# Half-slot order in a three-layer graph kernel: counts one half at a time, table remainders behind a maximum, VectorE's pieces half a slot behind their products

## The chip, the cores and the metric

The kernel runs on one core of one Trainium2 chip. The time is the device time of one execution in microseconds (us); the median of three runs counts. A core has a matrix engine (TensorE, PE in the profile), a vector engine (VectorE, DVE), a scalar engine (ScalarE, ACT), a general-purpose engine (GpSimd, POOL) and a queue engine for transfers (SyncE, SP). Each engine carries out its own instructions in order, and semaphores hold an instruction until what it reads or overwrites is ready. PSUM, where the matrix engine writes its products, has 8 banks of 512 float32 values per partition.

## The reference

Four layers work on 16 graphs of 1024 nodes with 128 features. Each is `x = layernorm(x + layer(x, adj))`.

- Layer 0 is attention over neighbours: relu of three linear maps, scores `q k^T` with non-neighbours pushed down by a penalty, a softmax, and a sum of `v`.
- Layer 1 is an edge convolution with a maximum over neighbours:

```python
p = jnp.einsum('bnd,do->bno', x, W1 - W2)
q = jnp.einsum('bnd,do->bno', x, W2)
pre = p[:, :, None, :] + q[:, None, :, :] + b
h = jax.nn.relu(pre) * adj[..., None]
return jnp.max(h, axis=2)
```

- Layer 2 adds up neighbours and applies a two-layer network with a relu.
- Layer 3 first thins out the adjacency row by row: a row with many neighbours loses every few of them, with the symmetric entries, so that later rows see what earlier ones removed (the dilation). Then come three mean aggregations with a normalisation of rows and batch statistics over all graphs, and a last linear map.

## The kernel before

The maximum over neighbours is the bulk of the work. It is the maximum of `q` over the neighbours, plus `p`. The kernel takes the source nodes of a graph in groups of 12 (`PS`), two sets of 6. For each set it makes a **table** of the maxima of `q` over all 64 subsets of the six nodes (`tables_of`, on VectorE, tile `sub`). Which subset a node sees is found by a product of the adjacency with signs (`count`, L701 to L709): TensorE counts matches into `pm` (L708), ScalarE turns that into a one-hot `hot` (L709). A second product of `hot` with the table picks the maximum out (`look_up`, L737, tile `pg`), and VectorE takes the running maximum over groups (`best`, L789 and L791). A table is cut into a rounded part `high` and a remainder `low`, and both are multiplied. So each table first goes through a transpose on TensorE (`pt`, L720), a cast on ScalarE (`high`, L722) and a subtraction on VectorE (`low`, L728), for two groups at once.

One graph has 86 groups (`NP`), and 16 graphs make 1376 **slots**, one group each. The order of the instructions on each engine is written out by this program itself (`slot`, from L749), not by a scheduler. A slot has two halves, of 512 nodes each. In each half it writes, in this order: four matmuls of the look-up, then what other **streams** have for TensorE, then what they have for the other engines (`advance`), and last the maximum. The counts and the table for the slot after next are written in the second half, behind the streams, both halves of the counts together. The subtraction `low` stands at the start of every odd slot.

The streams are generators: `scores` and `attend` (layer 0 and the products of layer 1 for the next graph), `rest` (end of layer 1 and layer 2 for the graph before), `tables_of`, and beside them `dilation`, which is paced by due times counted in slots. A stream yields what it wants next with `ask(engine, cost, ...)`. `advance` lets it go on if its engine has room, if the delay since its last step has passed, and, for a product (`take=True`), if one of two shared PSUM banks is free. The delay is half a slot, or none with `same=True`. A piece with `give=True` reads a product out of its bank, and the bank may be taken again half a slot later. The pieces of VectorE that the change touches read products in this way: `e` (scores, L330), `y` (L379, L396, L441) and `hT` (L420).

There are two PSUM pools of note. `wide` has two tiles of two banks for `pg`, so the look-up of one half waits until the maximum of two halves before has read its tile. `subset` has two banks, which `pm` and `pt` use in turn in the order in which they are asked for: three in an even slot and two in an odd one. The remainder `low` reads `pt` too, so `pt`'s bank comes free when `low` is done.

When the slots are over, the last pieces of the dilation and the aggregations of layer 3 follow, without slots.

Of the kernel before, what the change touches and what calls it, by code (L numbers as in the profile page):

```python
# [71 lines left out]
def tile_graph_layers(ctx: ExitStack, tc, a, out):  # L72
# [161 lines left out]
    def layers_012():  # L234
# [56 lines left out]
        def scores(b):  # L291

            if b > 1:
                yield ask("Pool", 0, after=("p", b - 1))
            if b > 2:
                yield ask("Pool", 0, after=("rest", b - 3))
            load_rows(b)
            xT = w4.tile([P, N], F32, name="xT")
            yield from columns_of(xT, X[b])
            qT = w4.tile([P, N], F32, name="qT")  # L300
            yield from product_of(WqT, xT, qT, AF.Relu, bq)
            kT = w4.tile([P, N], F32, name="kT")
            yield from product_of(WkT, xT, kT, AF.Relu, bk)
            v = values[b] = w4.tile([P, T, D], F32, name="v")
            for h in range(2):
                yield ask("PE", 1.1, take=True)
                pv = shared("pv").rearrange("p (t d) -> p t d", d=D)
                nc.tensor.matmul(pv, ones_b[:3, :], four(bv3), start=True, stop=False)
                for t in range(4):
                    nc.tensor.matmul(pv[:, t, :], xT[:, (4 * h + t) * P:(4 * h + t + 1) * P], WvT,  # L310
                                     start=False, stop=(t == 3))
                yield ask("A", 0.6, give=True, same=True)
                nc.scalar.activation(v[:, 4 * h:4 * h + 4, :], pv, AF.Relu)
            for t in range(T):

                yield ask("A", 1.05)
                off = w4.tile([P, N], BF, name="off", tag="pen")
                nc.scalar.activation(off, An[b][:, t, :], AF.Identity, bias=ones[:, 0:1], scale=-1.0)
                if t > 1:
                    yield ask("PE", 0, same=True, after=("back", b, t - 2))  # L320
                e = w4.tile([P, N], F32, name="e", bufs=2)

                tops = small.tile([P, 2], F32, name="tops")
                for h, s in enumerate(halves):
                    yield ask("PE", 1.07, take=True)
                    psc = shared("psc")
                    nc.tensor.matmul(psc, qT[:, t * P:(t + 1) * P], kT[:, s], start=True, stop=False)  # L327
                    nc.tensor.matmul(psc, penalty, off[:, s], start=False, stop=True)
                    yield ask("V", 0.66, give=True, same=True)
                    nc.vector.tensor_scalar(e[:, s], psc, CLAMP_HI, None, op0=ALU.min, op1=ALU.max,  # L330
                                            accum_out=tops[:, h:h + 1])
                yield ask("V", 0.1, same=True)
                top = small.tile([P, 1], F32, name="top")
                nc.vector.tensor_scalar(top, tops[:, 0:1], tops[:, 1:2], -1.0, op0=ALU.max, op1=ALU.mult)
                yield ask("A", 1.1)
                total = small.tile([P, 1], F32, name="total")
                nc.scalar.activation(e, e, AF.Exp, bias=top, accum_out=total)
                exps[b, t] = e, total
                happened["e", b, t] = now
            yield ask("A", 0.01, after=("X1", b), delay=0.5)  # L340
            xT = w4.tile([P, N], F32, name="xT1", tag="xT")
            yield from columns_of(xT, X[b])
            q = w4.tile([P, NP * PS], F32, name="q", bufs=2)
            nc.gpsimd.memset(q[:, N:], LOWEST)
            yield from product_of(W01[:, 1, :], xT, q[:, :N], None, None)
            qs[b] = q
            happened["q", b] = now
            if b > 1:
                yield ask("A", 0, same=True, after=("y1", b - 2))
            p = ps[b] = w4.tile([P, N], F32, name="p", bufs=2)  # L350
            yield from product_of(Wd, xT, p, AF.Identity, b01)
            happened["p", b] = now

        def attend(b):
            for t in range(T):
                yield ask("PE", 0.01, after=("e", b, t))
                if t == 0:
                    y = w4.tile([P, T, D], F32, name="y0", tag="xT")
                e, total = exps.pop((b, t))
                eT = w4.tile([P, T, P], F32, name="eT")  # L360
                for h in range(2):
                    yield ask("PE", 0.44, take=True, same=(h == 0))
                    p = shared("pe")
                    for c in range(4):
                        nc.tensor.transpose(p[:, c * P:(c + 1) * P],  # L365
                                            e[:, (4 * h + c) * P:(4 * h + c + 1) * P], ident)
                    yield ask("A", 0.59, give=True, same=True)
                    nc.scalar.copy(eT[:, 4 * h:4 * h + 4, :].rearrange("p c i -> p (c i)"), p)  # L368
                happened["back", b, t] = now
                for h in range(2):  # L370
                    yield ask("PE", 0.9, take=(h == 0))
                    if h == 0:
                        pav = shared("pav")[:, :D]
                    for c in range(4 * h, 4 * h + 4):
                        nc.tensor.matmul(pav, eT[:, c, :], values[b][:, c, :], start=(c == 0), stop=(c == T - 1))  # L375
                yield ask("V", 0.4, give=True, same=True)
                share = small.tile([P, 1], F32, name="share")
                nc.vector.reciprocal(share, total)
                nc.vector.scalar_tensor_tensor(y[:, t, :], pav, share, X[b][:, t, :], op0=ALU.mult, op1=ALU.add)  # L379
            yield from norm(X[b], y)  # L380
            happened["X1", b] = now


        def rest(b):
# [4 lines left out]
            for h in range(2):  # L389
                yield ask("PE", 0.44, take=True)  # L390
                pt = shared("ph")
                for t in range(4):
                    nc.tensor.transpose(pt[:, t * P:(t + 1) * P],
                                        best[:, (4 * h + t) * P:(4 * h + t + 1) * P], ident)
                yield ask("V", 0.66, give=True, same=True)
                nc.vector.tensor_add(y[:, 4 * h:4 * h + 4, :], X[b][:, 4 * h:4 * h + 4, :],  # L396
                                     pt.rearrange("p (t d) -> p t d", d=D))
            happened["y1", b] = now
# [12 lines left out]
            for h, s in enumerate(halves):  # L411
                for c in range(T):
                    yield ask("PE", 0.65, take=(c == 0), same=(c > 0))
                    if c == 0:
                        pa = shared("pa")
                    for k in range(3):
                        nc.tensor.matmul(pa, parts[:, k, c, :], An[b][:, c, s], start=(c == 0 and k == 0),  # L417
                                         stop=(c == T - 1 and k == 2))
                yield ask("V", 0.66, give=True, same=True)
                nc.vector.scalar_tensor_tensor(hT[:, s], xT[:, s], eps1, pa, op0=ALU.mult, op1=ALU.add)  # L420
            del An[b]
            zT = []
# [5 lines left out]
            for h in range(2):  # L428
                q = slice(4 * h, 4 * h + 4)
                for half in range(2):  # L430
# [4 lines left out]
                    for t in range(2 * half, 2 * half + 2):  # L435
                        own = slice((4 * h + t) * P, (4 * h + t + 1) * P)
                        for k in range(2):
                            nc.tensor.matmul(py[:, t, :], zT[k][:, own], W2[:, k, :],  # L438
                                             start=False, stop=(t == 3 and k == 1))
                yield ask("V", 0.65, give=True, same=True)  # L440
                nc.vector.tensor_mul(y[:, q, :], py, nm[:, q, b].unsqueeze(2).to_broadcast([P, 4, D]))  # L441
                yield ask("V", 0.65)
                nc.vector.tensor_add(y[:, q, :], y[:, q, :], X[b][:, q, :])
# [305 lines left out]
        def slot(s, last):  # L749
# [14 lines left out]
                    start(rest(b - 1))  # L764
            if s >= 0 and g % PC == 0:
                load_columns(b * (T + 1) + g // PC + 2)
            if s % 2 and s + 1 < last:
                low_part(s + 1)
            for h in range(2):
                now = s + 0.5 * h  # L770
                if s >= 0:
# [4 lines left out]
                if h == 0:  # L776
                    while s >= 0 and due <= s and not (wants_bank and taken >= 2 and given.get(taken - 2, 1e9) > now):
                        after, cost, wants_bank = next(dilate, (B * NP, 0, False))
                        due += after
                        room["V"] -= cost  # L780
                elif s + 2 < last:
                    for half in range(2):
                        count(s + 2, half)
                    if s % 2 == 0:
                        table(s + 2)
                if s >= 0:
                    own = bests[b][:, :, halves[h]]
                    if g == 0:
                        nc.vector.tensor_copy(own, pg)  # L789
                    else:  # L790
                        nc.vector.tensor_max(own, own, pg)  # L791
            if s >= 0:
                hots.pop(s)

# [24 lines left out]
        last = rest(B - 1)  # L819
# [310 lines left out]
```

## Time and profile before

Three runs took 7400.84, 7415.03 and 7416.94 us; the median is 7415.03 us. The profiled execution has a span of 7420.3 us at a mean granted TensorE clock of 0.856.

| engine | busy us | share of the span | instructions |
|---|---|---|---|
| TensorE matmuls | 5789.6 | 78% | 26554 |
| TensorE weight loads (beside matmuls) | 2790.6 | 38% | 26554 |
| VectorE | 5516.8 | 74% | 8427 |
| ScalarE | 3510.6 | 47% | 5849 |
| GpSimd | 3475.9 | 47% | 11285 |

| group | count | mean ns | busy us |
|---|---|---|---|
| VectorE `best`, L791 | 2720 | 1212 | 3226.8 |
| ScalarE `hot`, L709 | 2752 | 684 | 1740.9 |
| TensorE `pg` with `high` / with `low`, L737 | 5504 each | 549 / 445 | 1528.6 / 1247.6 |
| TensorE `pm`, L708 | 2752 | 432 | 953.7 |
| TensorE `pt`, L720 | 1376 | 331 | 337.3 |
| VectorE `low`, L728 | 688 | 421 | 289.9 |

To read it: the busy time of matmuls overlaps and their ends are modelled, so a share of 78% doesn't say how much is left. A group's idle time is what its engine stood still for just before it, and the engine named beside it is the one whose result came last. The slots run from about 130 us to 6090 us, the rest is the tail of layer 3. The chain of work that ended last is by engine TensorE 48%, VectorE 31%, ScalarE 10%.

### The profile page before, as it was taken

To read this page: it belongs to the slowest core of one execution; us is meant where nothing else is said; L and a number is where in the kernel's file an instruction comes from. 1 tells how busy PE (TensorE), PEld (TensorE's weight loads), DVE (VectorE), ACT (ScalarE), POOL (GpSimd) and SP (SyncE) were. 2 spreads that over 40 slices of the span, in tenths; PEclk is the share of its full clock that TensorE was granted. 3 is DMA by queue.
4 is the path that set the end of the run, shared out by engine and by line. 5 is a ranking of instruction groups with operands and counts; after the bars stand their busy time and mean duration, and the time that the engine had idled before them with its cause. 6 is when DMAs were issued, how large, how long until landed. Compare 5 with 4: busy or idle time off the path is not lost.

```text
span 7420.3 us, 84498 instructions
## 1 busy us (share of the span) xinstructions
PE 5789.6 (78%) x26554; PEld 2790.6 (38%) x26554; DVE 5516.8 (74%) x8427; ACT 3510.6 (47%) x5849; POOL 3475.9 (47%) x11285
## 2 busy tenths in 40 slices
PE   6768787777777777787778787878787767888996
PEld 3323333333333333333333333333333324555653
DVE  3888888888888888888888888888888774444443
ACT  3545455555454545454545454545454443333751
POOL 3454554545555555555555555555555551110116
PEclk8878888888888888888988888889888778888998
DMA  5121212121212121212121112121111025565544
GB/s 34 18 24 18 29 19 29 19 29 18 30 18 30 18 30 18 29 18 28 18 29 18 28 18 28 17 30 20 30 18 22 14 30 104 114 114 110 191 157 153
DMA packets 494372, 318.88 MB, mean 43 GB/s; under 512 B 316651, under 2 KB 445669, under 8 KB 489829
## 3 DMA queue, kind: packets, MB, share of 16 engines
q0 software_dynamic: 105648, 84.20, 13.1%
q1 hardware_dynamic: 383600, 228.10, 10.9%
q8 instruction: 211, 3.46, 0.2%
q10 hardware_dynamic: 4676, 1.19, 0.1%
q14 instruction: 237, 1.93, 0.1%
HBM read 413.70 MB, written 118.16 MB: 72 GB/s over the span
## 4 chain that ended last, share of the span: by engine, by line
PE 48%; DVE 31%; ACT 10%; issue 5%; POOL 4%; DMA 2%; ACTq 0%; DVEq 0%; SPq 0%; POOLq 0%
PE pg L737 15%; DVE best L791 13%; ACT hot L709 6%; PE pagg L910 5%; PE pm L708 4%; DVE rank L626 4%; PE pav L375 3%; PE psc L327 3%; PE pp L284 2%; PE pa L417 2%; PE pt L720 2%; DVE sub L465 2%; DVE gone L632 2%; PE pe L365 2%; PE py L438 1%
## 5 line engine op out<-in xcount | busy, mean ns | idle before, releaser
L791 DVE TENSOR_TENSOR best<-best,pg 128x1024 f32<-128x1024 f32 x2720 | 3226.8, 1212 | 266.3 <-PE pg L737 255.5
L709 ACT ACTIVATE hot<-pm,one_less 128x512 fp32r<-128x512 f32 x2752 | 1740.9, 684 | 1967.4 <-PE pm L708 1963.9
L737 PE MATMUL pg<-hot,high 64*128 64x512 f32 x5504 | 1528.6, 549 | 689.2 <-DVE best L791 609.5
L737 PE MATMUL pg<-hot,low 64*128 64x512 f32 x5504 | 1247.6, 445 | 0.0
L737 PEld LDWEIGHTS pg<-hot,high 64*128 64x128 f32 x5504 | 592.6, 207 | 1707.5 <-issue 589.3
L708 PE MATMUL pm<-AT,lit 120*128 120x512 fp8e4 x2752 | 953.7, 432 | 8.0 <-ACT hot L709 7.3
L720 PE MATMUL pt<-ident,sub 128*128 128x128 f32 x1376 | 337.3, 331 | 482.5 <-ACT hot L709 463.7
L737 PEld LDWEIGHTS pg<-hot,low 64*128 64x128 f32 x5504 | 624.4, 219 | 12.9
L728 DVE TENSOR_TENSOR low<-pt,high 128x256 fp32r<-128x256 f32 x688 | 289.9, 421 | 368.6 <-ACT high L722 364.6
L489 POOL DMA_DIRECT2D E<-in_adj_dram x128 | 70.8, 563 | 953.2 <-DVE gone L632 856.9
L577 POOL TENSOR_SCALAR sc<-low_counts,half_mask,rest 16x1 f32<-16x1 f32 x992 | 340.2, 343 | 301.7 <-DVE rest L563 207.5
L720 PEld LDWEIGHTS pt<-ident,sub 128*128 128x128 f32 x1376 | 151.2, 154 | 877.2 <-ACT hot L709 875.6
L582 POOL TENSOR_SCALAR sc<-sc 16x1 f32<-16x1 f32 x992 | 391.9, 395 | 104.7
L708 PEld LDWEIGHTS <-lit 120*128 120x128 fp8e4 x2752 | 200.6, 101 | 518.4 <-issue 500.0
L579 POOL TENSOR_SCALAR sc<-sc 16x1 f32<-16x1 f32 x992 | 318.8, 321 | 107.5
L584 POOL TENSOR_SCALAR hit<-V,sc 16x31 bf16<-16x31 bf16 (+30 forms) x992 | 361.3, 364 | 0.0
L409 POOL TENSOR_TENSOR left<-X,parts 128x1024 f32<-128x1024 f32 x16 | 34.1, 2133 | 674.3 <-ACT parts L406 674.3
L940 POOL TENSOR_TENSOR length<-length,mhalf 128x8 f32<-128x8 f32 x48 | 79.0, 1645 | 572.1 <-DVE length L939 572.1
L629 ACT ACTIVATE rank<-rank,centre,scale 128x1024 f32<-128x1024 f32 x128 | 158.7, 1240 | 392.5 <-DVE rank L626 392.5
L585 POOL TENSOR_SCALAR last_rank<-V,sc 16x31 f32<-16x31 bf16 (+30 forms) x992 | 337.5, 340 | 0.0
L465 DVE TENSOR_TENSOR sub<-sub,q 128x24 f32<-128x24 f32 (+11 forms) x768 | 316.4, 413 | 23.8 <-ACT q L287 10.5
L375 PE MATMUL pav<-v,eT 128*128 128x128 f32 x2048 | 317.3, 303 | 2.0 <-ACT eT L368 2.0
(242 smaller groups left out, 9498.9 us busy)
## 6 DMA issues: line engine op xcount, KB each, us to landing
removed<-gone SPq DMA_DIRECT2D x128, 256.0 KB
An<-in_adj_dram POOLq DMA_DIRECT2D x16, 1024.0 KB, 14.8
E<-in_adj_dram POOLq DMA_DIRECT2D x128, 128.0 KB, 6.4
gone_all<-removed POOLq DMA_DIRECT2D x64, 256.0 KB, 12.3
near<-in_adjT_dram POOLq DMA_DIRECT2D x16, 1024.0 KB, 17.4
h<-x SPq DMA_DIRECT2D x32, 512.0 KB
kept<-near SPq DMA_DIRECT2D x16, 1024.0 KB
share<-share SPq DMA_DIRECT2D x32, 512.0 KB
```

The source lines that it names most:

```text
L375: nc.tensor.matmul(pav, eT[:, c, :], values[b][:, c, :], start=(c == 0), stop=(c == T - 1))
L465: nc.vector.tensor_max(sub[:, :n_g, n:2 * n], sub[:, :n_g, 0:n], qg[:, 2 * g0:2 * g0 + n_g, k:k + 1].to_broadcast([P, n_g, n]))
L577: gp.tensor_scalar(half, mine, half_mask[:, m], rest[:, n:n + 1], op0=ALU.mult, op1=ALU.add)
L582: gp.tensor_scalar(to, at, sf, none, op0=ALU.subtract, op1=ALU.subtract)
L584: gp.tensor_scalar(hit[:, n, n + 1:], V[:, n, n + 1:], at, None, op0=ALU.is_equal)
L585: gp.tensor_scalar(last[:, n + 1:], V[:, n, n + 1:], to, None, op0=ALU.is_le)
L708: nc.tensor.matmul(pm, lit[:, r, :], AT[b * (T + 1) + c][:, halves[h]], start=True, stop=True)
L709: nc.scalar.activation(hots[s][:, halves[h]], pm, AF.Relu, bias=one_less)
L720: nc.tensor.transpose(pt[:, k * P:(k + 1) * P], subs[b, g0][:, g - g0 + k, :], ident)
L737: nc.tensor.matmul(pg[:, a], part[rows, at * P:(at + 1) * P], hots[s][rows, halves[h]], start=(k == 0), stop=(k == 1))
L791: nc.vector.tensor_max(own, own, pg)
L910: nc.tensor.matmul(pa[:, s], piece[:, c, :], m[c][:, s], start=(c == 0 and k == 0), stop=(c == T - 1 and k == 1))
```

## The change

It has three edits.

1. The counts for the slot after next are written one half at a time: the first behind the streams of the first half, the second behind those of the second half. Before, both stood in the second half. The table still comes behind the second count, in even slots.
2. The subtraction `low` in odd slots moves from the start of the slot to behind the maximum of its first half.
3. Five VectorE pieces that read a product lose `same=True`: they are written half a slot behind the product, so that the next look-up of TensorE stands between the two. The two shared banks are then given back half a slot later.

The aim is that no engine meets an instruction whose input was asked for only just before. No operation is added or taken away, and the arithmetic is the same.

```diff
--- before.py
+++ after.py
@@ -326,7 +326,7 @@
                     psc = shared("psc")
                     nc.tensor.matmul(psc, qT[:, t * P:(t + 1) * P], kT[:, s], start=True, stop=False)
                     nc.tensor.matmul(psc, penalty, off[:, s], start=False, stop=True)
-                    yield ask("V", 0.66, give=True, same=True)
+                    yield ask("V", 0.66, give=True)
                     nc.vector.tensor_scalar(e[:, s], psc, CLAMP_HI, None, op0=ALU.min, op1=ALU.max,
                                             accum_out=tops[:, h:h + 1])
                 yield ask("V", 0.1, same=True)
@@ -373,7 +373,7 @@
                         pav = shared("pav")[:, :D]
                     for c in range(4 * h, 4 * h + 4):
                         nc.tensor.matmul(pav, eT[:, c, :], values[b][:, c, :], start=(c == 0), stop=(c == T - 1))
-                yield ask("V", 0.4, give=True, same=True)
+                yield ask("V", 0.4, give=True)
                 share = small.tile([P, 1], F32, name="share")
                 nc.vector.reciprocal(share, total)
                 nc.vector.scalar_tensor_tensor(y[:, t, :], pav, share, X[b][:, t, :], op0=ALU.mult, op1=ALU.add)
@@ -392,7 +392,7 @@
                 for t in range(4):
                     nc.tensor.transpose(pt[:, t * P:(t + 1) * P],
                                         best[:, (4 * h + t) * P:(4 * h + t + 1) * P], ident)
-                yield ask("V", 0.66, give=True, same=True)
+                yield ask("V", 0.66, give=True)
                 nc.vector.tensor_add(y[:, 4 * h:4 * h + 4, :], X[b][:, 4 * h:4 * h + 4, :],
                                      pt.rearrange("p (t d) -> p t d", d=D))
             happened["y1", b] = now
@@ -416,7 +416,7 @@
                     for k in range(3):
                         nc.tensor.matmul(pa, parts[:, k, c, :], An[b][:, c, s], start=(c == 0 and k == 0),
                                          stop=(c == T - 1 and k == 2))
-                yield ask("V", 0.66, give=True, same=True)
+                yield ask("V", 0.66, give=True)
                 nc.vector.scalar_tensor_tensor(hT[:, s], xT[:, s], eps1, pa, op0=ALU.mult, op1=ALU.add)
             del An[b]
             zT = []
@@ -437,7 +437,7 @@
                         for k in range(2):
                             nc.tensor.matmul(py[:, t, :], zT[k][:, own], W2[:, k, :],
                                              start=False, stop=(t == 3 and k == 1))
-                yield ask("V", 0.65, give=True, same=True)
+                yield ask("V", 0.65, give=True)
                 nc.vector.tensor_mul(y[:, q, :], py, nm[:, q, b].unsqueeze(2).to_broadcast([P, 4, D]))
                 yield ask("V", 0.65)
                 nc.vector.tensor_add(y[:, q, :], y[:, q, :], X[b][:, q, :])
@@ -764,8 +764,6 @@
                     start(rest(b - 1))
             if s >= 0 and g % PC == 0:
                 load_columns(b * (T + 1) + g // PC + 2)
-            if s % 2 and s + 1 < last:
-                low_part(s + 1)
             for h in range(2):
                 now = s + 0.5 * h
                 if s >= 0:
@@ -778,10 +776,9 @@
                         after, cost, wants_bank = next(dilate, (B * NP, 0, False))
                         due += after
                         room["V"] -= cost
-                elif s + 2 < last:
-                    for half in range(2):
-                        count(s + 2, half)
-                    if s % 2 == 0:
+                if s + 2 < last:
+                    count(s + 2, h)
+                    if h and s % 2 == 0:
                         table(s + 2)
                 if s >= 0:
                     own = bests[b][:, :, halves[h]]
@@ -789,6 +786,8 @@
                         nc.vector.tensor_copy(own, pg)
                     else:
                         nc.vector.tensor_max(own, own, pg)
+                if h == 0 and s % 2 and s + 1 < last:
+                    low_part(s + 1)
             if s >= 0:
                 hots.pop(s)
```

## The prediction

> **What bounds the kernel now.** I read the page's slices first, then the waits of TensorE (PE) and of VectorE (DVE) over 200 to 5900 us, then one graph cut into twelve stretches, and last some 60 us instruction by instruction.
>
> The slices show that the slot loop (16 graphs of 86 slots) fills slices 1 to 33 at one steady level, and that neither PE nor DVE is full in it:
>
> ```profile
> PE   6768787777777777787778787878787767888996
> DVE  3888888888888888888888888888888774444443
> ...
> PEclk8878888888888888888988888889888778888998
> ```
>
> L744, which ends a graph, starts at 502.1 us the first time and at 6087.1 the last: 15 graphs in 5585 us, 372 us a graph, 4.33 us a slot. What follows 6090 us (1330 us of graph layers) is not touched by the change. In the four windows that make up 200 to 5900 us DVE is busy 4695 of 5700 us (1066.8 + 1232.5 + 1240.8 + 1155.5) and PE 4465. So DVE idles 1005 us and PE 1235 us while they pass work to and fro. Where these waits end:
>
> ```profile
> PE pg L737 <- DVE best L791: 575.1, 643, 11.0
> PE pt L720 <- ACT hot L709: 440.4, 624, 5.1
> ```
>
> ```profile
> DVE low L728 <- ACT high L722: 345.2, 343, 7.0
> DVE best L791 <- PE pg L737: 248.1, 282, 4.2
> DVE e L330 <- PE psc L328: 148.3, 143, 2.3
> DVE y L379 <- PE pav L375: 83.2, 88, 3.3
> DVE y L396 <- PE ph L393: 38.3, 23, 1.9
> DVE y L441 <- PE py L438: 31.8, 24, 2.9
> DVE hT L420 <- PE pa L417: 27.0, 29, 1.2
> ```
>
> (Columns: us in total, times, longest.) PE's second largest wait is the transposes of the tables, 440 us in 624 of the roughly 660 pairs in the window. DVE's largest is the subtraction `low`, 345 us. The waits of DVE pieces on products that PE was given in the same half slot are 148.3 + 83.2 + 38.3 + 31.8 + 27.0 = 328.6 us.
>
> The timeline at 3457 us shows that the first two are one loss seen from both sides: the two counts end, ScalarE (ACT) turns both into `hot`, only then does `pt` get its bank, then `high`, then `low`, while DVE has nothing else it may do:
>
> ```profile
> 3456.51 1.26 ACT L709 ACTIVATE hot<-pm,one_less 128x512 fp32r<-128x512 f32 x2
> ...
> 3457.24 0.44 PE L720 MATMUL pt<-ident,sub 128*128 128x128 f32 x2 [0.92 <-ACT hot L709]
> ...
> 3457.72 0.37 ACT L722 CAST high<-pt 128x256 fp32r<-128x256 f32 x1
> ...
> 3458.12 0.42 DVE L728 TENSOR_TENSOR low<-pt,high 128x256 fp32r<-128x256 f32 x1 [1.37 <-ACT high L722]
> ```
>
> The chain that ended last agrees: ACT `hot` L709 has 6% of the span on it, some 445 us, though ACT is busy for only 47%. That is the detour over ACT.
>
> **What the Trainium skill says.** "TensorE: Matmul & The Clock Gate", section "Architectural detail", has ACT and DVE as strict first-in first-out, and PE's matmuls in program order with only weight loads pulled ahead. So a waiting `low` holds every `best` behind it, and a waiting `pt` holds every `pg`; the two waits above agree. "Perfetto Trace Analysis", section "Matmuls", wants independent matmul groups to rotate through PSUM banks so that one's evacuation lies beside the next one's matmuls; two counts and a table in succession through two banks don't do that, 440 us of `pt` waits say. The first page's "Part 1: The HAM clock gate" has the PE clock halved after an idle window; here one graph shows a clock of 0.50 where PE is busy 17.13 of 31 us and 1.00 where it is busy 27.43 of 31. "SBUF — State Buffer", section "Who interferes with whom", has a DVE instruction with two SBUF inputs contend with a GpSimd instruction that reads SBUF; an L585 beside a DVE `sub` took 0.72 us where its neighbours took 0.33.
>
> **Part 1: counts one half at a time, and `low` behind the first maximum.** The work is the same; the order is new. Subset banks alternate in order of allocation: three in an even slot (count, count, table), two in an odd one. Before, `pt` took the bank of a count issued just ahead of it, so it had to sit through that count's 0.69 us `hot`. Now the first count lies half a slot earlier, with a `pg` group (0.66 us on the chain) and perhaps a product between; its `hot` is over when `pt` comes. Whole run: `pt` waited 463.7 us, `low` 364.6. They are the same loss, so I don't add them. From below, 0: where another wait takes its place. From above, 464. What is left when it goes: in stretches where DVE is full (3483 to 3514 us, busy 30.72 of 31) nothing is won, since `low` waits only as long as DVE would be waited for elsewhere. In one such pair of stretches, 3452 to 3514, PE waits 15.5 us for `best` against 4.9 for `pt`. I take two thirds: **-300 us**.
>
> What it adds: (a) `pt`'s bank is held until `low`, which now lies behind the first maximum of the odd slot (1.21 us, L791); the odd slot's second count takes that bank, and behind it on PE queues the next slot's `pg`. But that `pg` needs this very maximum read out of its own bank, so `low` can add at most its own 0.42 us: between 0 and 688 x 0.42 = 290 us. PE has a `pg` group and a count between, about 0.9 us and often a product, against 1.63 us of maximum and `low`, so it waits only where DVE is behind. There DVE still has the second maximum (1.21 us) to run while PE does the count (0.27 on the chain) and the `pg` (0.66), so it hardly idles. I take **+40**. (b) PE changes once more per slot between 120-row counts and 64-row look-ups. The first, `high`, matmuls of a group have a median of 496 ns against 393 for `low`, so a change costs 0 to 0.10 us, 0 to 140 us in 1376 slots. I take **+40**. `low` itself is early enough for its look-up: two maxima later.
>
> **Part 2: VectorE's pieces half a slot behind their products.** The piece (`e`, 690 ns; `y`, 351; `hT`, 747) goes into DVE's queue ahead of the next half's maximum instead of this half's. PE has by then had a `pg` in between, so the 328.6 us of waits largely end. In stretches that PE bounds this wins nothing: from 3358 to 3421 us DVE waits 6.7 us for `pg` anyhow, out of some 14 us idle. From below 0, from above 328.6; I take half, **-165**. The price: a shared bank is held half a slot longer, and each score tile's sequence of two products grows by about a slot, eight slots a graph. No engine does more work by that. But `q`, near 3452 us in a graph that ends at 3514, gets later and the tables of the next graph with it, so transposes may wait for `sub`: 0 to 3 us per graph, 48 us at most. I take **+20**.
>
> Sum: -300 + 40 + 40 - 165 + 20 = -365, and 7415 - 365 = **7050 us**. A slot falls from 4.33 to about 4.07 us. DVE would be busy 4695 of about 5350 us, 88%. GpSimd's row of the dilation (ten operations, whose means add up to 2.86 us; starts 3.3 to 3.8 us apart in the timeline, once 4.2) is paced at 0.9 slot, 3.66 us then, so it is not yet the bound, and 7.3 slots of slack lie ahead of the wait for its result.
>
> **The rivals.**
> A, everything is won: both losses go whole and the denser PE keeps its clock: -364.6 - 328.6 = -693, 6720 us. For it: DVE could hold 4695 us of work in the time, and low clock sits where PE idles. Against: `pg` waits of 248 us on DVE grow once DVE runs ahead, and PE-bound stretches (28.96 of 32 us at 3389) have only 3 us to give. 15%.
> B, the waits change name: `pt`'s wait turns into PE waiting for `best`, already the largest, or DVE's waits become `best` on `pg`; a quarter of 465 + a quarter of 329 is won, less the 100 of costs: 7415 - 198 + 100 = about 7315 us. For it: 575 us of `best` waits; against: two engines at 78 and 82% with a shared detour of 0.7 us every two slots. 18%.
> C, slower: `low` behind the maximum stalls the counts for the whole 290 us, the changes of rows cost 140, the late tables 48, and only B's 198 is won: 7415 + 280 = 7695 us at worst, some 7500 in the middle. For it: every PE stall is also a stall of all later look-ups, and lowers the clock. Against: the argument under (a). 7%.
>
> **How the numbers follow.** My forecast has 60%, A 15%, B 18%, C 7%. Costs and gains of the forecast, each moved by half, span 6900 to 7200. The range takes in that, part of A and nearly all of B: 6830 to 7310. Slower by over 0.2%: C and a shred of B, 8%; within 0.2%: 4%; faster: 88%.
>
> **What would show it.** Right: `pt` <- `hot` under 150 us in total; `low` <- `high` under 80; the `e`, `y` and `hT` waits under 100 together; `best` <- `pg` larger than 248; PE's `pg` <- `best` about as before; ACT `hot` under 3% of the chain; clock at or above 0.86; PE counts waiting for `low` under 60 us. Wrong: a new wait `pm` <- `low` in the hundreds, `pt` <- `sub`, GpSimd's rows on the chain, or PE waiting for `best` by as much as `pt` gave up.

## The result and the profile after

The changed kernel takes 6987.95 us (median of four runs, 6986.96 to 6989.2) against 7412.17 us before (median of four, one more than in the table ahead): a ratio of 0.943, 95% interval 0.9414 to 0.9446, some 424 us less. The forecast was 7050 us in 6830 to 7310.

The page's slices, as shown of the kernel before:

```profile
PE   6878797978797878787878787878787867887996
...
DVE  3989898989898989898989898989898854444453
...
PEclk8879898889897979897989898989897778888998
```

DVE now has 8 and 9 in turn where 8 stood before. L744 runs from 476.5 to 5657.2 us: 345.4 us a graph, 4.02 us a slot (4.33 before). In 190 to 5480 us, which cuts off the loop's ends as 200 to 5900 did, DVE is busy 4697 us of 5290, 89%. Its work was 4695 us before, so the gain is idle time: 1005 us then, 593 now.

The waits of TensorE, in that window:

```profile
PE pg L737 <- DVE best L788: 424.6, 468, 16.1
PE pm L708 <- ACT hot L709: 260.7, 113, 8.2
PE pt L720 <- ACT hot L709: 86.1, 92, 3.0
```

The second of these was small before, in 200 to 5900 us:

```profile
PE pm L708 <- ACT hot L709: 6.1, 1, 6.1
```

And of VectorE (`best` is L788 here, L791 before):

```profile
DVE best L788 <- PE pg L737: 472.8, 595, 9.4
DVE best L786 <- PE pg L737: 16.4, 12, 1.4
DVE hit_T L598 <- DMA hit_p<-hit: 14.5, 2, 13.9
DVE low_counts L561 <- PE pc L557: 9.5, 6, 2.5
DVE e L330 <- PE psc L328: 8.6, 17, 0.9
DVE low L728 <- ACT high L722: 8.6, 3, 6.0
DVE y L396 <- PE ph L393: 2.1, 4, 0.7
```

The transposes' wait fell from 440 to 86 us, `low`'s from 345 to 9, and the five product waits from 329 to 11. Two things are new. `best` waits longer for `pg` (248 to 473 us), which was expected of a VectorE that runs ahead. And counts wait 261 us for `hot`, which was not. The chain of the whole span, before and after, shows a new engine on it:

```profile
PE 48%; DVE 31%; ACT 10%; issue 5%; POOL 4%; DMA 2%; ACTq 0%; DVEq 0%; SPq 0%; POOLq 0%
```

```profile
PE 31%; DVE 28%; POOL 23%; issue 9%; ACT 4%; DMA 2%; ACTq 0%; SPq 0%; DVEq 0%; POOLq 0%
```

ScalarE fell from 10 to 4%, and `hot` is not among the lines of 2% or more, as foreseen. But GpSimd went from 4 to 23%. One way from GpSimd to the counts leads over a layer norm: GpSimd works out its factors (`ln_mv`, L217 to L226), among its rows of the dilation, and ScalarE applies them (`X`, L268). ScalarE's wait for them over the whole span, before and after:

```profile
ACT X L268 <- POOL ln_mv L226: 23.7, 4, 10.7
```

```profile
ACT X L268 <- POOL ln_mv L226: 129.3, 22, 10.7
```

The timeline shows one such wait, of a kind that comes once a graph, some 346 us apart, and lasts 4 to 7.5 us. (Columns: start and length in us, engine, line, operation; in brackets how long the engine stood still just before, and what ended that.)

```profile
4223.69 0.10 PEld L708 LDWEIGHTS <-lit 120*128 120x128 fp8e4 x1 [0.37 <-issue]
...
4224.30 0.20 POOL L217 TENSOR_TENSOR ln_mv<-ln_st 128x8 f32<-128x8 f32 x1
...
4226.07 1.66 POOL L225 TENSOR_TENSOR ln_mv<-ln_mv,mhalf 128x8 f32<-128x8 f32 x1
4227.81 0.20 POOL L226 TENSOR_TENSOR ln_mv<-ln_mv 128x8 f32<-128x8 f32 x1
...
4228.04 2.80 ACT L268 ACTIVATE X<-y,ln_mv 128x128 f32<-128x128 f32 x7 [7.15 <-POOL ln_mv L226]
...
4230.75 0.67 ACT L709 ACTIVATE hot<-pm,one_less 128x512 fp32r<-128x512 f32 x1
...
4231.47 0.58 PE L708 MATMUL pm<-AT,lit 120*128 120x512 fp8e4 x1 [7.70 <-ACT hot L709]
...
4234.31 1.22 DVE L788 TENSOR_TENSOR best<-best,pg 128x1024 f32<-128x1024 f32 x1 [9.07 <-PE pg L737]
```

Read from the top: TensorE loads the count's weights at 4223.7 us, and the count itself must wait. GpSimd reaches the factors at 4224.3 us. ScalarE stands at `X`, which needs them, from 4220.9 to 4228.0. `hot` stands behind `X`, the next count behind `hot`'s bank, `pg` behind the count, and VectorE idles 9.07 us. This is one cause of the counts' wait, not the whole of it; the experiments show a second.

### The profile page after: what moved, and what is told of

It reads as the page before. It is cut to its first block, busy times and chain, and to the rows that moved or that the text cites. A ratio compares the mean times of both kernels' runs of the same rounds, so it can differ in the third digit from the quotient of the medians.

```text
span 6986.7 us, 84240 instructions
## 1 busy us (share of the span) xinstructions
PE 5721.4 (82%) x26554; PEld 2797.7 (40%) x26554; DVE 5508.9 (79%) x8427; ACT 3566.9 (51%) x5849; POOL 3478.3 (50%) x11285
## 4 chain that ended last, share of the span: by engine, by line
PE 31%; DVE 28%; POOL 23%; issue 9%; ACT 4%; DMA 2%; ACTq 0%; SPq 0%; DVEq 0%; POOLq 0%
DVE best L788 12%; PE pg L737 8%; PE pagg L909 5%; DVE rank L626 4%; PE pm L708 3%; POOL sc L582 3%; DVE sub L465 2%; POOL sc L577 2%; POOL hit L584 2%; POOL last_rank L585 2%; POOL sc L579 2%; DVE gone L632 2%; PE pp L284 2%; POOL sc L578 2%; POOL sc L580 2%
## 5 line engine op out<-in xcount | busy, mean ns | idle before, releaser
L788 DVE TENSOR_TENSOR best<-best,pg 128x1024 f32<-128x1024 f32 x2720 | 3249.6, 1212 | 495.7 <-PE pg L737 489.1
L709 ACT ACTIVATE hot<-pm,one_less 128x512 fp32r<-128x512 f32 x2752 | 1877.9, 686 | 1495.1 <-PE pm L708 1492.1
L708 PE MATMUL pm<-AT,lit 120*128 120x512 fp8e4 x2752 | 1164.0, 423 | 289.8 <-ACT hot L709 269.0
L737 PE MATMUL pg<-hot,low 64*128 64x512 f32 x5504 | 1222.1, 441 | 0.0
L737 PEld LDWEIGHTS pg<-hot,high 64*128 64x128 f32 x5504 | 563.1, 201 | 1572.6 <-DVE best L788 1036.1
L737 PEld LDWEIGHTS pg<-hot,low 64*128 64x128 f32 x5504 | 590.7, 211 | 29.4 <-DVE low L728 0.6
L708 PEld LDWEIGHTS <-lit 120*128 120x128 fp8e4 x2752 | 274.2, 100 | 795.7 <-issue 762.4
L720 PE MATMUL pt<-ident,sub 128*128 128x128 f32 x1376 | 307.7, 309 | 94.0 <-ACT hot L709 91.7
L629 ACT ACTIVATE rank<-rank,centre,scale 128x1024 f32<-128x1024 f32 x128 | 158.7, 1240 | 408.0 <-DVE rank L626 407.9
L720 PEld LDWEIGHTS pt<-ident,sub 128*128 128x128 f32 x1376 | 190.2, 155 | 328.5 <-ACT hot L709 251.5
L896 ACT CAST m<-near 128x1024 fp32r<-128x1024 fp8e4 x256 | 253.3, 1045 | 112.5 <-DVE near L865 59.7
L327 PE MATMUL psc<-kT,qT 128*128 128x512 f32 x512 | 297.3, 664 | 0.0
```

Source lines behind the costliest of these rows:

```text
L708: nc.tensor.matmul(pm, lit[:, r, :], AT[b * (T + 1) + c][:, halves[h]], start=True, stop=True)
L709: nc.scalar.activation(hots[s][:, halves[h]], pm, AF.Relu, bias=one_less)
L720: nc.tensor.transpose(pt[:, k * P:(k + 1) * P], subs[b, g0][:, g - g0 + k, :], ident)
L737: nc.tensor.matmul(pg[:, a], part[rows, at * P:(at + 1) * P], hots[s][rows, halves[h]], start=(k == 0), stop=(k == 1))
```

## The experiments

Each run was timed beside new runs of the kernel before, whose median lay between 7404.58 and 7415.44 us. Differences between experiments are therefore sure to some 10 us only; the ratios are each to the kernel before of the same time.

**Each part alone.** The first has the counts and the move of `low`, with the pieces back beside their products:

```diff
-                    yield ask("V", 0.66, give=True)
+                    yield ask("V", 0.66, give=True, same=True)
...
```

> The changed kernel with its VectorE pieces back in the half slot of their products (the five same=True), so only the counts one half at a time and the subtraction behind the first maximum are new. Theory of the prediction (two separate gains, 300 less 80 of costs for this part): 7412 - 220 = about 7190 us; waits of transposes for hot under 150 us, product waits of VectorE still near 330 us. Rival, one gain only (this part alone removes the detour over ScalarE, the product waits merely hide it): within 60 us of the changed kernel's 6988. Rival, the parts need each other (nothing here because VectorE still stops at products): over 7350.

Measured: 7128.24 us, ratio 0.9616 (0.9601 to 0.963), 284 us less than the 7411.99 before it. The transposes' wait is 88 us over the span, the waits for `psc` and `pav` are still 163 and 156 us. The gain is 62 us more than forecast for this part.

The second is the kernel before with the later pieces alone.

> The kernel before with only its five VectorE pieces half a slot later; counts together and the subtraction at the start of odd slots as before. Theory of the prediction: 7412 - 145 = about 7267 us, product waits of VectorE under 100 us, transposes still waiting some 440 us for hot. Rival, the product waits only change their name to maximum waiting for look-up: within 30 us of 7412. Rival, late streams cost: over 7430.

Measured: 7298.44 us, ratio 0.9847 (0.9832 to 0.9861), 114 us less. The waits for `psc` and `pav` fell from 172 and 122 to 37 and 35 us, the transposes still wait 481 us, and `low` now waits 578 us for `high` instead of 365: part of what the pieces gave up was passed on there, and the gain is 31 us short of the forecast. So both parts gain by themselves: 284 + 114 = 398 of the 424 us. Neither rival that made one of them all or nothing holds.

**The two edits of the first part.** First the changed kernel with `low` back at the start of odd slots:

```diff
+            if s % 2 and s + 1 < last:
+                low_part(s + 1)
             for h in range(2):
...
-                if h == 0 and s % 2 and s + 1 < last:
-                    low_part(s + 1)
```

> The changed kernel with the subtraction back at the start of odd slots, ahead of the first maximum. Theory of the prediction (the move costs 40 us because the second count of odd slots waits for it, and the wait of low for high is gone anyway once the transposes don't wait): about 6950 us, low waiting for high under 100 us. Rival (the move is what frees VectorE: high comes after the start of the slot in any case, so VectorE stands until transposes, cast and subtraction are through): 7050 us or more, low waiting for high over 200 us.

Measured: 7053.12 us, ratio 0.9516 (0.9502 to 0.953), 65 us slower than the changed kernel. The rival was right; in this kernel's waits of VectorE, over the whole span:

```profile
DVE low L728 <- ACT high L722: 339.2, 279, 8.7
```

The transposes wait only 69 us for `hot` in it, so the wait of `low` doesn't depend on theirs.

Next, both counts in the second half again, with the other edits kept:

```diff
-                if s + 2 < last:
-                    count(s + 2, h)
-                    if h and s % 2 == 0:
+                if h and s + 2 < last:
+                    for half in range(2):
+                        count(s + 2, half)
+                    if s % 2 == 0:
                         table(s + 2)
```

> The changed kernel with both counts in the second half of the slot again; subtraction behind the first maximum and pieces half a slot later as in the change. Theory of the prediction (the transposes' wait for hot is the loss, seen on TensorE): waits of transposes back near 440 us, some 200 to 300 us slower than the changed kernel, 7190 to 7290. Rival (it is VectorE's wait for the subtraction that counted, and that is hidden by the move alone): under 7060.

Measured: 7225.38 us, ratio 0.9747 (0.9731 to 0.9764), 237 us slower than the changed kernel; the transposes wait 471 us for `hot` again, while `low` waits for `high` 1 us. The split of the counts is the largest single piece, and the move of `low` alone doesn't do its work. Part of the 237 us is a wait that only this combination has: counts wait for `low`, 105 us in 153 waits, against 0.7 us in the changed kernel. With `low` at the start of the slot the split is free of that, and is worth 245 us (7298.44 to 7053.12).

**GpSimd as the new bound.** Five runs slow its rows or move the norm's use of its factors. A row every 1.0 slot:

```diff
-                    yield 0.9, 0.06, False
+                    yield 1.0, 0.06, False
...
-                yield B * NP / K - 35.66, 0, False
+                yield B * NP / K - 38.76, 0, False
```

> The changed kernel with GpSimd's rows of the dilation written every 1.0 slot instead of 0.9, and the wait ahead of their result shortened by as much (35.66 to 38.76 taken off), so that the dilation's blocks keep their length in slots. Theory now (at 4.02 us a slot GpSimd's queue runs behind; a layer norm's factors stand behind its rows, ScalarE waits for them, hot behind it, the counts on TensorE behind hot): ScalarE's wait for the factors falls from 129 us to about 20, the counts' wait for hot from 269 to about 120, and the time by 60 to 130 us to 6860 to 6930. Rival (GpSimd's place on the chain is only where the trace follows a tie; TensorE and VectorE bound the slots): within 20 us of 6988. Rival (the dilation's later result collides with its deadline): over 7010.

Measured: 6948.36 us, ratio 0.938 (0.9367 to 0.9393), 40 us less than the changed kernel, and short of the 60 that the theory asked for. ScalarE's wait for factors fell to 22 us as stated, but the counts' wait for `hot` only halved, to 136 us. VectorE's wait for the dilation's result (`hit_T`) rose from 24 to 89 us, since the slower rows eat the slack ahead of it.

> As the run with 1.0, but 0.95 slot (37.21 taken off). Theory: 0.95 of 4.02 us is 3.82 us, over the 3.3 to 3.7 us that a row takes, so most of the gain is there: between 6870 and 6950 us. Rival (no bound by GpSimd): within 20 us of 6988.

Measured: 6942.33 us, ratio 0.9374 (0.9361 to 0.9387), 46 us less, inside the theory's span. The wait for factors is 67 us, that for the result 69. The two paces can't be told apart in time (their intervals overlap). GpSimd has 29% of the chain here and 23% in the slower changed kernel, so its share of the chain doesn't measure the loss.

> The changed kernel with ScalarE's first application of a layer norm six slots behind the request for its factors instead of four; GpSimd's own work and pace are as in the changed kernel. Theory (the loss is ScalarE standing at late factors with hot behind it): ScalarE's wait for factors falls from 129 us to under 50 and the time by 30 to 100 us. Rival (the wait for factors is hidden, or the streams that come two slots later cost as much): within 20 us of 6988.

The edit is `delay=6` for `delay=4` in `norm`. Measured: 6965.77 us, ratio 0.9403 (0.939 to 0.9416), 22 us less: short of the 30 that the theory set, and hardly outside the rival's 20. Its interval touches the changed kernel's, so the time decides neither. The wait for factors fell to 36 us as stated, and that for the dilation's result rose to 80.

> The kernel before with GpSimd's rows every 1.0 slot. Theory (at 4.33 us a slot 0.9 slot is 3.90 us and GpSimd has slack, as ScalarE's 24 us of waits for factors say): within 20 us of 7412. Rival (a slower pace is simply better for VectorE and TensorE, whatever the slot): 60 us or more faster, which would take the run with 1.0 slot away as a proof.

Measured: 7471.55 us, ratio 1.0087 (1.0069 to 1.0105), 67 us slower, which neither expected. What it does decide is that the slower pace is no gain by itself: it costs 67 us at 4.33 us a slot and saves 40 at 4.02. The loss lies in the slots: the last graph ends at 6153.1 us, 66 later. It is spread over many waits, of which TensorE's for `best` grew most, from 609 to 652 us; why isn't settled.

> The changed kernel with rows every 0.95 slot and the norm's application six slots behind the request: both single edits in one, which gave 46 and 22 us each. Theory (one loss, GpSimd late with the factors, met from two ends): the sum isn't reached, 6915 to 6945 us, ScalarE's wait for factors under 30 us. Rival (two separate losses): 6920 or less, at most 6925. The VectorE wait for the dilation's result, 69 and 80 us in the single runs, should rise if the later streams feed it.

Measured: 6966.12 us, ratio 0.9396 (0.9383 to 0.9409): no faster than either edit alone, and 24 us slower than the pace alone (16 by the ratios, whose intervals just overlap). Both expected times were missed, while the waits came as stated: that for factors fell to 21 us, and that for the dilation's result rose:

```profile
DVE hit_T L598 <- DMA hit_p<-hit: 156.5, 26, 16.3
```

The dilation is a ring of its own (counts, 31 rows on GpSimd, transfers, ranks on VectorE, next counts) that must close in 43 slots. Reordering round it moved the wait from ScalarE to VectorE in these runs.

So a further run made the rows themselves shorter, at the old pace. It leaves out part of the computation, as its expectation says:

```diff
-                    gp.tensor_scalar(to, at, sf, none, op0=ALU.subtract, op1=ALU.subtract)
-                    last = small.tile([B, R], F32, name="last_rank")
                     gp.tensor_scalar(hit[:, n, n + 1:], V[:, n, n + 1:], at, None, op0=ALU.is_equal)
-                    gp.tensor_scalar(last[:, n + 1:], V[:, n, n + 1:], to, None, op0=ALU.is_le)
-                    gp.tensor_add(hit[:, n, n + 1:], hit[:, n, n + 1:], last[:, n + 1:])
```

> The changed kernel with seven instead of ten GpSimd operations in each row of the dilation: it leaves out the second of the two neighbours classes that a row removes (the ranks beyond the last full step), so the thinned graph isn't the reference's; all other instructions, their order and the 0.9 slot are kept. A row then takes about 2.4 us instead of 3.35 us. Theory (GpSimd, not its pace in slots, is the bound that came in place of the old ones, by late factors for ScalarE and a late result for VectorE): ScalarE's wait for factors under 40 us and VectorE's wait for the dilation's result under 20 us both at once, which neither the slower pace nor the later norm could do, and 6870 to 6935 us. Rival (TensorE and VectorE bound the slots, the waits for GpSimd are hidden): within 25 us of 6988.

Measured: 6823.66 us, ratio 0.9201 (0.9188 to 0.9213), 164 us less than the changed kernel and more than the theory's span. Both waits are gone at once, as stated: 18 us for factors, and none for the result among its waits. Its chain:

```profile
PE 45%; DVE 38%; issue 7%; ACT 5%; POOL 2%; DMA 1%; ACTq 0%; DVEq 0%; POOLq 0%; SPq 0%
```

GpSimd is back at 2%. So three small operations per row cost the changed kernel 164 us, though GpSimd is busy half of its span. How much of that goes by ScalarE and how much by the dilation's result isn't told apart. Slower VectorE instructions beside GpSimd's, which the prediction names, are no visible part: VectorE is busy 5504.0 us here and 5508.9 in the changed kernel. The kernel before wasn't run with lighter rows, so it isn't shown that the whole 164 us are new with the change.

The run also shows the second cause of the counts' wait, because late factors are gone and the wait is not (its lines from L586 on are four lower: L704 is L708, L705 is L709, L625 is L629):

```profile
PE pm L704 <- ACT hot L705: 153.7, 113, 4.4
```

```profile
2470.18 1.24 ACT L625 ACTIVATE rank<-rank,centre,scale 128x1024 f32<-128x1024 f32 x1 [5.70 <-DVE rank L622]
...
2471.32 0.67 ACT L705 ACTIVATE hot<-pm,one_less 128x512 fp32r<-128x512 f32 x1
2472.04 0.59 PE L704 MATMUL pm<-AT,lit 120*128 120x512 fp8e4 x1 [4.39 <-ACT hot L705]
```

Here `hot` stands behind the dilation's `rank` on ScalarE, and `rank` behind two scans of VectorE. The first part alone has this too: counts wait 166 us there, with 28 us for factors. So some 150 of the changed kernel's 269 us over the span need no late factors.

**Counts ahead of the streams.** Two last kernels put each count right behind its look-up, so that `hot` stands ahead of ScalarE's pieces of the same half:

```diff
+                if s + 2 < last:
+                    count(s + 2, h)
                 advance(("PE",))
...
-                if s + 2 < last:
-                    count(s + 2, h)
-                    if h and s % 2 == 0:
-                        table(s + 2)
+                if s + 2 < last and h and s % 2 == 0:
+                    table(s + 2)
```

> The changed kernel with the count of each half written right behind the look-up, ahead of the streams' products and of ScalarE's pieces; the table stays behind them. Theory (ScalarE's queue is what is left of the counts' wait: hot stands behind pieces that wait for late factors): with hot ahead of the pieces of its half, the counts' wait for hot falls from 269 us to under 180 and the time by 20 to 80 us. Rival (a piece that stands still holds the next half's hot in any case, and the streams' products come a count later): within 20 us of 6988. Rival (products later and hot waiting for a younger count delay ScalarE's other pieces): over 7010.

Measured: 6939.85 us, ratio 0.9354 (0.9342 to 0.9367), 48 us less, as the theory has it. The counts' wait for `hot` fell from 269 to 21 us, though ScalarE still waits 97 us for factors. `pg`'s wait for `best` rose from 455 to 695.

> The same with GpSimd's rows every 0.95 slot (6942 us without this edit). Theory: the pace has already removed half of ScalarE's waits for factors, so 0 to 40 us are left: 6900 to 6945. Rival: over 6950.

Measured: 6934.26 us, ratio 0.935 (0.9337 to 0.9363). The two intervals overlap: the pace adds nothing that can be measured once `hot` is ahead. By their medians these two are the fastest kernels here that compute everything, about 50 us ahead of the change; the interval of the 0.95 pace alone overlaps both.

## Why the prediction was right, and where it wasn't

- **Two rings with a shared detour over ScalarE, not a full engine**: shown. VectorE's work is the same to 2 us and its idle time fell by 412 us, which is nearly the whole difference. With the counts together again, the transposes' wait for `hot` is back at 471 us and the kernel 237 us slower.
- **`pt` and `low` are one loss, 300 us of it to be won**: near in size, wrong in kind. The first part gave 284 us by itself and 310 on top of the second (7298.44 to 6987.95), where 220 were forecast once (a) and (b) are taken off. But each wait stands without the other: `low` waits 339 us where the transposes wait 69, and the transposes 471 us where `low` waits 1. With the later pieces in place, the split alone is worth 245 us and the move of `low` alone 73 (7298.44 to 7053.12 and to 7225.38), nearly the 310 together, so they are two losses rather than one. What holds is that the waits don't add up to a gain: they were 481 and 578 us there.
- **Term (a), `low` behind the maximum costs 40 us**: wrong in sign. The move is worth 65 us on top of the split. The bound of the step held (the count's wait for `low` is 0.7 us, not 290), but I had taken `low`'s own wait to vanish with the transposes'. It doesn't: with `low` at the start of an odd slot, `high` still stands behind the second `hot` on ScalarE, which is busy with `hot` for 171 of the 339 us of waits that remain.
- **Term (b), changes of rows, 40 us**: not seen in the durations. The `high` matmuls of a look-up have a median of 497 ns after and 496 before, the mean is 550 against 549.
- **Product waits worth half of 329 us, late tables 20 us**: 114 us alone, and 140 on top of the first part (7128.24 to 6987.95), against 145 net. No cost of late tables is seen: transposes wait for `sub` 1.1 us in all.
- **GpSimd is not yet the bound at 0.9 slot**: this failed. I compared a row's 3.3 to 3.8 us with a pace of 3.66 us and left out what else stands in that queue: the factors of a norm (3.7 us from L217 at 4224.30 to the next row) and the issue of loads (0.6 to 0.7 us each). At 0.9 slot of 4.02 us the pace is 3.61 us, and the queue falls behind: the 31 rows of one block start between 4125.74 and 4241.80 us, 3.87 us apart on average. ScalarE stands behind it.

The costs in my sum, 100 us, came out at about -65, and it left GpSimd's 164 us out: with lighter rows the gain is 588 us (7412.17 to 6823.66), where 365 were forecast. These errors stood against each other, so that the total came as near as it did is in part luck. Of the eight signs for it seven came (`pg`'s wait for `best` fell by 150 us rather than stayed), and of those against it one, GpSimd's rows on the chain. Rival B, waits that change name, is partly true: 225 us of the gain in waits came back as `best` on `pg`. The range's upper end, 7310 us, lies below that rival's own 7315, so it took in about half of B, not nearly all.

## What to carry to other kernels

When two in-order engines each idle for a fifth of the time, look for the instruction whose input is asked for just ahead of it on another engine, and write half a stage between the two. Don't add up the waits that the two engines show: here 481 and 578 us of them gave 310. Ask of each engine with a pace of its own what the shorter stage leaves of its slack, with everything that shares its queue: here three of the ten operations of a row, on an engine at 50%, cost 164 us. Put the work that feeds the main ring ahead of side work in each queue, so that a late side result holds it less; that was worth some 50 us here.

## What the hardware showed

A stall costs more than its length. The count that ends the 7.70 us wait at 4231.47 us takes 0.58 us, and the first pairs of the look-ups after it take 0.79 and 0.80 us; just before the stall they took 0.39 and 0.50. Counts still take 0.63 us at 4237.73, six microseconds on. The granted clock is 1.00 in the 4.7 us before the stall, 0.50 from 4231.4 to 4237.4 us, and 1.00 again from 4240. That agrees with the clock gate of the Trainium skill's page "TensorE: Matmul & The Clock Gate", "Part 1", which halves the clock after an idle window and needs a busy one to restore it.

Over the whole span the mean clock moved little (0.856 to 0.863), and the transposes' median from 328 to 273 ns, without any change to them; no run shows why.
